# The end of a two-layer graph attention kernel: where the last weights are summed, where the first layer's rows are added, and in which order the last products run

## The chip, the cores and the metric

The kernel runs on one core of a Trainium2 chip. A core has TensorE (PE) for matrix products into PSUM, VectorE (DVE), ScalarE (ACT) and GpSimd (POOL) for everything elementwise, and SyncE (SP), which here issues DMAs. Each engine works through its own queue of instructions in order; semaphores make one engine wait for another. The metric is the device time of one execution in microseconds, as the median of several runs.

## The reference, cut to what matters

Two attention layers over a graph of 4096 nodes with 512 features. Each layer adds its input to its output and normalises every row. Only the second layer's end is touched here:

```python
q = jnp.einsum('nd,hdk->hnk', node_matrix, Wqs)
k = jnp.einsum('nd,hdk->hnk', node_matrix, Wks)
v = jnp.einsum('nd,hdk->hnk', node_matrix, Wvs)
scores = jnp.einsum('hqk,hmk->hqm', q, k) * kd ** (-0.5)
scores = scores + IDENTITY_BIAS * eye - MASK_VAL * (1.0 - adj)
att = jax.nn.softmax(scores, axis=-1)
return jnp.einsum('hqm,hmk,hko->qo', att, v, Wo)
...
x = _layernorm(x + _L1_gnn_ref(x, adj, ...), axis=-1)
```

There are 8 heads of 64 features. The softmax's denominator is a sum over all 4096 nodes, for every head and every row.

## The kernel before, in words

The second layer works on pairs of heads and groups of 512 rows: 8 groups `g` times 4 pairs of heads `m` give 32 `pairs`, and each runs over 32 tiles `j` of 128 neighbours. For one `(g, m, j)` TensorE computes the scores of 128 neighbours against 512 rows for two heads (`score`, L1138), ScalarE takes the exponential (L1549), and VectorE multiplies with the mask (L1552), which gives the weight tile `p`, 128 by 1024. Then TensorE multiplies `p` with the values into an accumulator `o` in PSUM (`products`, L1597). `step` takes up to three tiles `j` at once: it issues the scores of this batch, the weighing of this batch, and the products of the batch before.

The denominators need the sum of all 32 weight tiles of a pair. `add_up` plans it: for two neighbouring tiles either a DMA adds one onto the other (L1582) and GpSimd adds the result to `q_sum` (L1572), or GpSimd adds both. The plan is carried out later, by `Later`: `later.at(n, fn)` calls `fn` at the n-th `later.step()` from then on, and every `step` ends with one `later.step()`. Instructions stand in the engines' queues in the order in which this Python code issues them; nothing reorders them. At the end of a pair TensorE sums `q_sum` over the partitions with a matrix of ones, and the result's reciprocal is multiplied onto `o` (`divide`, or `divide_at_once` for the last pair), giving `on`. When a group's four pairs are done, `project` multiplies `on` with the output weights (four products per tile of 128 rows, one for each `m`), and `close1` adds the first layer's rows `y` (loaded by `load_y`), takes the row's mean and variance (`normal_factors`: two VectorE instructions, L510 and L512, then four small ones on GpSimd, L514 to L519), normalises on ScalarE (L1676) and writes the tile out.

In the last pair the ten weight tiles from `j` = 22 on are not given to GpSimd but put in the list `last_sum`. After the last batch VectorE adds six of these into one (five instructions, L1729) and TensorE sums the remaining four itself, together with `q_sum` and VectorE's sum (`all_sums`, L1603). At that point five tiles of rows are open: `tiles[-5]`, of the group before, and the four of the last group. Of these four, the products for `m` = 0, 1 and 2 can run early, and only the last one needs the last pair's `on`. The kernel also tests that all sums are in range (`all_in_range`), counts the partitions for which this holds with a tiny matrix product, and reads the number; if it is not 128, a general version would run.

PSUM has three buffers for scores (`s_ps`), which the last tiles' results use too, and one for `o` (`o1_ps`).

Of the kernel before, what the change touches and what calls it, by code (L numbers as in the profile page):

```python
# [13 lines left out]
ALU = mybir.AluOpType  # L14
# [415 lines left out]
def tile_gat_then_masked_attention(  # L430
# [91 lines left out]
    def all_in_range():  # L522
# [3 lines left out]
        for n, op in ((0, ALU.max), (2, ALU.min)):  # L526
            nc.vector.tensor_reduce(ends[:, 2 + n:4 + n],
                                    span[:, :, n:n + 2].rearrange("p g k -> p k g"), AX.X, op)
        nc.vector.tensor_reduce(ends[:, 0:1], total, AX.X, ALU.add)
        nc.vector.tensor_reduce(ends[:, 1:2], most, AX.X, ALU.add)  # L530
        for n, (value, limit, op) in enumerate((
                (ends[:, 2:3], F_MAX, ALU.is_le), (ends[:, 3:4], F_MAX, ALU.is_le),
                (ends[:, 4:5], -F_MAX, ALU.is_ge), (ends[:, 5:6], -F_MAX, ALU.is_ge),
                (ends[:, 0:1], SUM_MAX, ALU.is_le), (ends[:, 1:2], 1.0 / SUM_MIN, ALU.is_le))):
            nc.vector.tensor_scalar(ok[:, n:n + 1], value, limit, None, op0=op)
# [561 lines left out]
    with wait_by_tile("l1", 1) as l1, wait_by_tile("l1a", 2) as lp, \  # L1097
# [415 lines left out]
        with wait_by_tile("l1w", 2) as wp, wait_by_tile("l1o", 1, space=PSUM) as op:  # L1513
# [42 lines left out]
            def add_up(g, m, j):  # L1556
# [19 lines left out]
                elif at_end and i >= n - 5:  # L1576
                    last_sum.extend((a, b))
# [7 lines left out]
            last_sum = []  # L1585

# [72 lines left out]
            def project(g, t, s, ms=range(NP1)):  # L1659
                for m in ms:  # L1660
                    nc.tensor.matmul(s, on_t[g][:, m, t * P:(t + 1) * P], wo_sb[:, m, :],  # L1661
                                     start=(m == 0), stop=(m == NP1 - 1))
# [17 lines left out]

# [8 lines left out]
            def step(batch, extra_sum, extra_tile, wait=4):  # L1689
# [15 lines left out]
                for u in batch:  # L1705
                    add_up(*u)
                for g, m, j in last:
                    products(g, m, j)
# [6 lines left out]
                last[:] = batch  # L1715
                later.step()

            for n, (g, m) in enumerate(pairs):
                for js in per_pair if n + 1 < len(pairs) else last_pair:
# [4 lines left out]
            for t in tiles[-5:]:  # L1724
                load_y(*t)
            step([], None, None)
            later.step()
            for p in last_sum[1:-4]:
                nc.vector.tensor_tensor(last_sum[0], last_sum[0], p, op=ALU.add)  # L1729
            step([], None, tiles[-5], 2)  # L1730
            y_ps = ps.tile([P, HP, G], F32, name="s_ps")
            den_ps = ps.tile([P, HP, G], F32, name="s_ps")
            o_ps = op.tile([P, 2, G], F32, name="o1_ps")
            y_ps = [y_ps[:, 0, :], y_ps[:, 1, :], o_ps[:, 0, :], o_ps[:, 1, :]]
            for n in range(2):
                project(*tiles[n - GT], y_ps[n], range(NP1 - 1))
            all_sums([q_sum.pop(pairs[-1]), last_sum[0]] + last_sum[-4:], den_ps[:, 0, :])
# [52 lines left out]
```

## Time and profile before

| what | value |
|---|---|
| median of 3 runs (lowest to highest) | 3330.91 us (3329.23 to 3331.56) |
| profiled execution | 3330.41 us, span 3328.3 us |
| TensorE busy | 3301.2 us, 99% of the span |
| VectorE busy | 2484.2 us, 75% |
| GpSimd busy | 2167.3 us, 65% |
| ScalarE busy | 1949.1 us, 59% |
| GpSimd sum `q_sum<-q_sum,p` (L1572) | 538 times, mean 2561 ns |
| VectorE weighing `p<-s_ps,adjT` (L1552) | 896 times, mean 1217 ns |
| last score products end | 3286.8 us |
| last result on ScalarE begins | 3320.87 us |

The span runs from the first to the last instruction of the core; the execution's own time is somewhat longer. A group of instructions is named by its line in the kernel, the engine, the operation, and the tiles it writes and reads (`out<-in`). PEld is TensorE's loading of weights, which overlaps its products; one product of 32-bit numbers shows as two records. A record's duration begins when the instruction is issued to the engine[...]. "PEclk" is the granted clock of TensorE, 1.00 being full.

### The profile page before, as it was taken

The numbers are of one execution on the slowest core, as the hardware profiler recorded it, in microseconds if no ns is written. First come the engines' busy times: TensorE is split into PE (matmuls) and PEld (weight loads), VectorE is DVE, ScalarE is ACT, GpSimd is POOL, SyncE is SP. The second block draws the span as 40 slices with busy tenths as digits, with TensorE's granted clock in tenths as the row PEclk, the third lists the DMA queues.
The fourth block names the chain that finished last, engine by engine and source line by source line (L and its number), as shares of the span: only waits on it lengthen the run. The fifth ranks groups of instructions, "written<-read, shape, count | busy, mean of one in ns | idle before, by whom it ended". The sixth has DMA issues, their size and how long they took to land.

```text
span 3328.3 us, 67210 instructions
## 1 busy us (share of the span) xinstructions
PE 3301.2 (99%) x27160; PEld 1965.5 (59%) x27160; DVE 2484.2 (75%) x3189; ACT 1949.1 (59%) x2439; POOL 2167.3 (65%) x1599
## 2 busy tenths in 40 slices
PE   9999999999999999999999999999999999999998
PEld 8899999999999777733333333333333333333333
DVE  6789899899999676567767676676766767667676
ACT  1267868878776310156656556566565656656554
POOL 5630040040030243389999999999999999999996
PEclk9999999999999999999999999999999999999999
DMA  8988796686532443489888988879888799887984
GB/s 180 227 204 183 219 187 169 152 184 146 137 93 58 111 149 114 149 223 205 191 211 226 224 202 191 210 188 257 203 194 212 186 214 244 194 210 186 213 196 112
DMA packets 398992, 612.04 MB, mean 184 GB/s; under 512 B 167632, under 2 KB 248528, under 8 KB 398672
## 3 DMA queue, kind: packets, MB, share of 16 engines
q0 software_dynamic: 97520, 258.77, 42.6%
q1 hardware_dynamic: 299280, 345.88, 33.5%
q8 instruction: 215, 3.52, 0.4%
q10 hardware_dynamic: 1872, 3.02, 0.4%
q14 instruction: 105, 0.86, 0.1%
HBM read 315.87 MB, written 109.25 MB: 128 GB/s over the span
## 4 chain that ended last, share of the span: by engine, by line
PE 92%; POOL 3%; DMA 2%; DVE 1%; issue 1%; ACT 0%; ACTq 0%; POOLq 0%; DVEq 0%
PE o_ps L1087 27%; PE o_ps L1597 24%; PE s_ps L1138 24%; PE o_ps L846 5%; PE s_ps L1661 3%; PE s_ps L1298 2%; PE s_ps L1255 2%; DMA p<-p 2%; PE s_ps L1248 1%; PE x_ps L1255 1%; POOL q_sum L1572 1%; PE x_ps L1248 1%; PE s_ps L1616 1%; POOL p L1582 0%; POOL adjT L1214 0%
## 5 line engine op out<-in xcount | busy, mean ns | idle before, releaser
L1572 POOL TENSOR_TENSOR q_sum<-q_sum,p 128x1024 f32<-128x1024 f32 x538 | 1378.0, 2561 | 64.0 <-DMA p<-p 38.2
L1552 DVE TENSOR_TENSOR p<-s_ps,adjT 128x1024 f32<-128x1024 f32 x896 | 1043.9, 1217 | 470.1 <-ACT s_ps L1549 438.4
L1549 ACT ACTIVATE s_ps<-s_ps 128x1024 f32<-128x1024 f32 x1021 | 967.5, 1006 | 597.3 <-PE s_ps L1138 594.2
L1138 PE MATMUL s_ps<-q_sb,k_sb 64*64 64x512 f32 x8192 | 943.5, 589 | 2.8 <-DVE p L1552 2.7
L1597 PE MATMUL o_ps<-p,v_sb 64*64 64x512 f32 x8192 | 943.6, 590 | 0.0
L1087 PE MATMUL o_ps<-sup_t,p 128*128 128x129 f32 x8192 | 915.7, 275 | 1.2 <-DVE p L640 1.2
L1087 PEld LDWEIGHTS o_ps<-sup_t,p 128*128 128x128 f32 x8192 | 915.3, 192 | 1.7 <-DVE p L640 1.4
L640 DVE SCALAR_TENSOR_TENSOR p<-fr_t,dj,az 128x1024 f32<-128x1024 f32 x512 | 650.2, 1284 | 66.1 <-PE o_ps L1087 37.9
L1138 PEld LDWEIGHTS s_ps<-q_sb,k_sb 64*64 64x64 f32 x8192 | 312.4, 133 | 569.9 <-issue 453.7
L1597 PEld LDWEIGHTS o_ps<-p,v_sb 64*64 64x64 f32 x8192 | 310.2, 133 | 570.7 <-issue 560.4
L624 ACT ACTIVATE z<-fr_t,f 128x1024 fp8e4<-128x1024 f32 x512 | 557.9, 1146 | 102.1 <-DVE az L635 101.8
L1582 POOL DMA_DIRECT2D p<-p x412 | 438.4, 1302 | 10.1 <-PE o_ps L1597 9.2
L1063 POOL DMA_DIRECT2D agg<-base_d x32 | 29.1, 1217 | 386.8 <-DMA sup_t<-sup_d 204.7
L585 POOL COPY seen<-token 128x1 f32<-128x1 f32 x24 | 10.9, 455 | 356.8 <-DVE token L583 356.8
L1552 DVE TENSOR_TENSOR p<-s_ps,md 128x1024 f32<-128x1024 f32 x128 | 150.8, 1218 | 67.0 <-ACT s_ps L1549 63.6
L635 DVE TENSOR_TENSOR az<-adjT,z 128x512 int32<-128x512 int32 x256 | 175.4, 685 | 2.9 <-ACT z L624 1.8
L600 ACT ACTIVATE adjT<-stage 128x1024 fp8e4<-128x1024 bf16 x128 | 131.2, 1055 | 17.0 <-DMA stage<-adj_d 16.7
L1661 PE MATMUL s_ps<-wo_sb,on 128*128 128x512 f32 x240 | 110.8, 604 | 0.0
L1631 ACT ACTIVATE r<-r_h 32x256 f32<-32x256 f32 x248 | 102.3, 413 | 2.9
L1277 POOL TENSOR_TENSOR v_sb<-v_sb,p 128x1024 f32<-128x1024 f32 x8 | 20.6, 2569 | 95.9 <-DVE v_sb L1283 52.4
L1049 ACT ACTIVATE agg<-o_ps,rinv 128x128 f32<-128x128 f32 x128 | 42.0, 370 | 69.8 <-DVE den L1042 45.9
L1322 ACT ACTIVATE v<-s_ps 128x256 f32<-128x256 f32 x28 | 10.8, 384 | 117.6 <-PE s_ps L1298 102.5
(274 smaller groups left out, 2257.3 us busy)
## 6 DMA issues: line engine op xcount, KB each, us to landing
p<-p POOLq DMA_DIRECT2D x412, 512.0 KB, 9.1
k_sb<-k_d SPq DMA_DIRECT2D x128, 512.0 KB
v_sb<-v_d SPq DMA_DIRECT2D x128, 512.0 KB
adj_d<-in_adj_dram POOLq DMA_DIRECT2D x32, 1024.0 KB, 11.0
sup_t<-sup_d SPq DMA_DIRECT2D x120, 258.0 KB
fr_t<-fr_d SPq DMA_DIRECT2D x16, 1024.0 KB
adjT_d<-adjT SPq DMA_DIRECT2D x32, 512.0 KB
adjT<-adjT_d SPq DMA_DIRECT2D x32, 512.0 KB
```

The lines of the kernel that those rows point to most:

```text
L624: nc.scalar.activation(z[:, k, :], fr_t[w, h][:, 0, :], AF.Sign, bias=fs[j // GT][:, 0, (j + k) % GT, h:h + 1], saturate=False)
L635: nc.vector.tensor_tensor(az.bitcast(I32), adjT[w, j // CJ][:, j % CJ:j % CJ + 2, :].bitcast(I32), z.bitcast(I32), op=ALU.bitwise_and)
L640: nc.vector.scalar_tensor_tensor(p, fr[:, 1, :], dj[j // GT][:, j % GT, h:h + 1], az_t[w, h, j // 2][:, j % 2, :], op0=ALU.max, op1=ALU.mult)
L846: nc.tensor.matmul(out[:, t * HD:(t + 1) * HD], xb[:, c, t * P:(t + 1) * P], wb[:, c, :], start=not more and t == 0 and c == 0, stop=c == ...
L1087: nc.tensor.matmul(o[t // BK][:, t % BK, :], p[:, t * P:(t + 1) * P], s, start=(j == 0 and t % BK == 0), stop=(j == NT - 1), skip_group_ch ...
L1138: nc.tensor.matmul(s[c:c + MS, e, :], k[r, a + c:a + c + MS], qt[g, m][r, :], start=True, stop=True)
L1549: nc.scalar.activation(s, s, AF.Exp, scale=float(KD) ** -0.5)
L1552: nc.vector.tensor_tensor(p, s, keep[:, None, :].to_broadcast([P, HP, G]), op=ALU.mult)
L1572: nc.gpsimd.tensor_tensor(q, q, p, op=ALU.add)
L1582: later.at(2, lambda: nc.gpsimd.dma_start(a, b, accum_op=ALU.add))
L1597: nc.tensor.matmul(o[c, n, :], v[r, j % CH, c], p[r, e, :], start=(j == 0), stop=(j == NT - 1))
L1661: nc.tensor.matmul(s, on_t[g][:, m, t * P:(t + 1) * P], wo_sb[:, m, :], start=(m == 0), stop=(m == NP1 - 1))
```

## The change

Four things change, all behind the last weighings or near them.

1. The list `last_sum` is summed by `gather` on VectorE: one sum after the second-last batch, five after the last batch is weighed, two more after the last pair's products. The last weight tile of all (`j` = 31) is left out of these and added to `q_sum` on GpSimd, planned five steps later by `add_up`. TensorE then sums only `q_sum` and the gathered tile.
2. The first layer's rows of the last four tiles are copied by ScalarE into the PSUM accumulators, and `project` adds its products onto them (`onto`); `close_in_place` therefore has no addition of `y`, takes mean and variance from PSUM, and normalises from PSUM, the last tile on VectorE and the others on ScalarE.
3. The products of `tiles[-5]` now come before the last pair's products, and the parts of the last four tiles are interleaved with their last products in another order. The closing of `tiles[-5]` comes after the gathering.
4. The range test is cut in two: what is known early is tested before the last sums (`in_range_so_far`), the rest after the first of the four tiles has been closed. Four of the five loads of `y` are issued two steps earlier, the fifth where it was.

```diff
--- before.py
+++ after.py
@@ -519,20 +519,26 @@
         nc.gpsimd.tensor_scalar(nb, nb, -1.0, None, op0=ALU.mult)
         return rs, nb
 
-    def all_in_range():
+    def in_range_so_far():
 
         ok = small.tile([P, 8], F32, name="ok")
         ends = small.tile([P, 6], F32, name="ends")
         for n, op in ((0, ALU.max), (2, ALU.min)):
             nc.vector.tensor_reduce(ends[:, 2 + n:4 + n],
                                     span[:, :, n:n + 2].rearrange("p g k -> p k g"), AX.X, op)
+        for n, (value, limit, op) in enumerate((
+                (ends[:, 2:3], F_MAX, ALU.is_le), (ends[:, 3:4], F_MAX, ALU.is_le),
+                (ends[:, 4:5], -F_MAX, ALU.is_ge), (ends[:, 5:6], -F_MAX, ALU.is_ge))):
+            nc.vector.tensor_scalar(ok[:, n:n + 1], value, limit, None, op0=op)
+        return ok, ends
+
+    def all_in_range(known):
+
+        ok, ends = known
         nc.vector.tensor_reduce(ends[:, 0:1], total, AX.X, ALU.add)
         nc.vector.tensor_reduce(ends[:, 1:2], most, AX.X, ALU.add)
-        for n, (value, limit, op) in enumerate((
-                (ends[:, 2:3], F_MAX, ALU.is_le), (ends[:, 3:4], F_MAX, ALU.is_le),
-                (ends[:, 4:5], -F_MAX, ALU.is_ge), (ends[:, 5:6], -F_MAX, ALU.is_ge),
-                (ends[:, 0:1], SUM_MAX, ALU.is_le), (ends[:, 1:2], 1.0 / SUM_MIN, ALU.is_le))):
-            nc.vector.tensor_scalar(ok[:, n:n + 1], value, limit, None, op0=op)
+        for n, value, limit in ((4, ends[:, 0:1], SUM_MAX), (5, ends[:, 1:2], 1.0 / SUM_MIN)):
+            nc.vector.tensor_scalar(ok[:, n:n + 1], value, limit, None, op0=ALU.is_le)
         all_ok = small.tile([P, 1], F32, name="all_ok")
         nc.vector.tensor_reduce(all_ok, ok[:, 0:6], AX.X, ALU.min)
         return all_ok
@@ -1574,6 +1580,8 @@
                 if i == 0:
                     later.at(1, first)
                 elif at_end and i >= n - 5:
+                    if j == NT - 1:
+                        later.at(5, lambda: add(b))
                     last_sum.extend((a, b))
                 elif i % 8 == 7:
                     later.at(2, lambda: add(a))
@@ -1583,6 +1591,11 @@
                     later.at(5, lambda: add(a))
 
             last_sum = []
+
+            def gather(count):
+                for p in last_sum[1:1 + count]:
+                    nc.vector.tensor_tensor(last_sum[0], last_sum[0], p, op=ALU.add)
+                del last_sum[1:1 + count]
 
             def products(g, m, j):
                 if j == 0:
@@ -1656,10 +1669,11 @@
                     den = wp.tile([P, G], F32, name="den1", bufs=1)
                     nc.scalar.activation(den, src, AF.Copy, accum_out=sums[:, n:n + 1])
 
-            def project(g, t, s, ms=range(NP1)):
+            def project(g, t, s, ms=range(NP1), onto=False):
                 for m in ms:
                     nc.tensor.matmul(s, on_t[g][:, m, t * P:(t + 1) * P], wo_sb[:, m, :],
-                                     start=(m == 0), stop=(m == NP1 - 1))
+                                     start=(m == 0 and not onto), stop=(m == NP1 - 1),
+                                     skip_group_check=onto)
 
             def load_y(g, t):
                 y_t[g, t] = wp.tile([P, D], F32, name="y1", bufs=5)
@@ -1677,7 +1691,25 @@
                     nc.sync.dma_start(out[i * P:(i + 1) * P, :], y)
                 later.at(wait, normalise)
 
-
+            def close_in_place(g, t, s, vector=False):
+                i = g * GT + t
+                y = y_t.pop((g, t))
+                st = small.tile([P, 6], F32, name="bn_st")
+                nc.vector.bn_stats(st, s)
+                mv = small.tile([P, 2], F32, name="bn_mv")
+                nc.vector.bn_aggr(mv, st)
+                rs = small.tile([P, 1], F32, name="bn_rs")
+                nc.gpsimd.tensor_scalar(rs, mv[:, 1:2], EPS, None, op0=ALU.add)
+                nc.gpsimd.tensor_tensor(rs, rs, minus_half, op=ALU.pow)
+                if vector:
+                    nc.vector.tensor_scalar(y, s, mv[:, 0:1], rs, op0=ALU.subtract,
+                                            op1=ALU.mult)
+                else:
+                    nb = small.tile([P, 1], F32, name="bn_nb")
+                    nc.gpsimd.tensor_tensor(nb, mv[:, 0:1], rs, op=ALU.mult)
+                    nc.gpsimd.tensor_scalar(nb, nb, -1.0, None, op0=ALU.mult)
+                    nc.scalar.activation(y, s, AF.Identity, bias=nb, scale=rs)
+                nc.sync.dma_start(out[i * P:(i + 1) * P, :], y)
 
             per_pair = [list(range(j, min(j + NB, NT))) for j in range(0, NT, NB)]
             n_short = 5
@@ -1704,6 +1736,11 @@
                     divide(*extra_sum, extra[:, 0, :])
                 for u in batch:
                     add_up(*u)
+                all_products()
+                last[:] = batch
+                later.step()
+
+            def all_products():
                 for g, m, j in last:
                     products(g, m, j)
                 for g, m, j in last:
@@ -1712,44 +1749,65 @@
                         o = o_t.pop((g, m))
                         nc.scalar.activation(o_sb[g, m], o[:, 0, :], AF.Copy)
                         nc.vector.tensor_tensor(o_sb[g, m], o_sb[g, m], o[:, 1, :], op=ALU.add)
-                last[:] = batch
-                later.step()
 
             for n, (g, m) in enumerate(pairs):
-                for js in per_pair if n + 1 < len(pairs) else last_pair:
+                for k, js in enumerate(per_pair if n + 1 < len(pairs) else last_pair):
                     whole = len(js) == NB
                     step([(g, m, j) for j in js],
                          None if whole or n < 1 else pairs[n - 1],
                          None if whole or n < NP1 + 1 else tiles[n - NP1 - 1])
-            for t in tiles[-5:]:
-                load_y(*t)
-            step([], None, None)
+                    if n + 1 == len(pairs):
+                        left = len(last_pair) - 1 - k
+                        if left == 2:
+                            for t in tiles[-5:-1]:
+                                load_y(*t)
+                        elif left == 0:
+                            load_y(*tiles[-1])
+                        elif left == 1:
+                            gather(1)
+            extra = ps.tile([P, HP, G], F32, name="s_ps")
+            project(*tiles[-5], extra[:, 1, :])
+            y_ps = ps.tile([P, HP, G], F32, name="s_ps")
+            y_ps = [y_ps[:, 0, :], y_ps[:, 1, :]]
+            for n in range(2):
+                nc.scalar.activation(y_ps[n], y_t[tiles[n - GT]], AF.Copy)
+            gather(5)
+            all_products()
             later.step()
-            for p in last_sum[1:-4]:
-                nc.vector.tensor_tensor(last_sum[0], last_sum[0], p, op=ALU.add)
-            step([], None, tiles[-5], 2)
-            y_ps = ps.tile([P, HP, G], F32, name="s_ps")
+            gather(len(last_sum) - 2)
+            close1(*tiles[-5], extra[:, 1, :], 2)
             den_ps = ps.tile([P, HP, G], F32, name="s_ps")
             o_ps = op.tile([P, 2, G], F32, name="o1_ps")
-            y_ps = [y_ps[:, 0, :], y_ps[:, 1, :], o_ps[:, 0, :], o_ps[:, 1, :]]
-            for n in range(2):
-                project(*tiles[n - GT], y_ps[n], range(NP1 - 1))
-            all_sums([q_sum.pop(pairs[-1]), last_sum[0]] + last_sum[-4:], den_ps[:, 0, :])
+            y_ps += [o_ps[:, 0, :], o_ps[:, 1, :]]
+            for n in range(2, GT):
+                nc.scalar.activation(y_ps[n], y_t[tiles[n - GT]], AF.Copy)
+            for _ in range(5):
+                later.step()
+            known = in_range_so_far()
+
+            def part(n):
+                project(*tiles[n - GT], y_ps[n], range(NP1 - 1), onto=True)
+
+            def rest(n):
+                project(*tiles[n - GT], y_ps[n], [NP1 - 1], onto=True)
+
+            part(0)
+            part(1)
+            all_sums([q_sum.pop(pairs[-1]), last_sum[0]], den_ps[:, 0, :])
             divide_at_once(*pairs[-1], den_ps[:, 0, :])
-            for n in range(GT):
-                if n + 2 < GT:
-                    project(*tiles[n + 2 - GT], y_ps[n + 2], range(NP1 - 1))
-                project(*tiles[n - GT], y_ps[n], [NP1 - 1])
-                if n == GT - 2:
-                    continue
-                if n == GT - 1:
-                    all_ok = all_in_range()
-                    close1(*tiles[n - 1 - GT], y_ps[n - 1], 1)
-                close1(*tiles[n - GT], y_ps[n], 1)
-                later.step()
-            count = den_ps[0:1, 1, 0:1]
-            nc.tensor.matmul(count, all_ok, ones[:, 0:1], start=True, stop=True)
-            nc.vector.tensor_copy(counted, count)
+            part(2)
+            rest(0)
+            part(3)
+            close_in_place(*tiles[-GT], y_ps[0])
+            all_ok = all_in_range(known)
+            for n in range(1, GT):
+                rest(n)
+                if n == 1:
+                    count = den_ps[0:1, 1, 0:1]
+                    nc.tensor.matmul(count, all_ok, ones[:, 0:1], start=True, stop=True)
+                close_in_place(*tiles[n - GT], y_ps[n], n == GT - 1)
+                if n == 1:
+                    nc.vector.tensor_copy(counted, count)
             later.flush()
```

## The prediction, made before the changed kernel was run

> **What bounds the kernel now.** The page's table of engines and its chain of work come first. TensorE is busy for almost the whole span and holds 92% of the chain, so nothing but the end of the kernel, where TensorE stops being the bound, can be moved by this change.
>
> ```profile
> span 3328.3 us, 67210 instructions
> PE 3301.2 (99%) x27160; PEld 1965.5 (59%) x27160; DVE 2484.2 (75%) x3189; ACT 1949.1 (59%) x2439; POOL 2167.3 (65%) x1599
> PE 92%; POOL 3%; DMA 2%; DVE 1%; issue 1%; ACT 0%; ACTq 0%; POOLq 0%; DVEq 0%
> ```
>
> Next, the same chain in order of time for the last 67 us (start, us, what). TensorE carries it to 3292.0; then it is VectorE's five sums of the last weights (L1729), TensorE's sums over them (L1603), TensorE's last products (L1661), and from 3313.7 VectorE, GpSimd and ScalarE closing the last tiles.
>
> ```profile
> 3286.83 5.20 PE o_ps L1597 x48
> ...
> 3292.68 0.69 DVE o_sb L1714
> 3293.36 1.62 DVE p L1729
> ...
> 3295.01 3.26 DVE p L1729
> ...
> 3302.09 4.50 PE s_ps L1603 x40
> 3306.59 2.77 PE o_ps L1661 x6
> ...
> 3320.33 0.19 POOL bn_nb L518
> ...
> 3320.87 0.81 ACT y L1676
> ```
>
> The last ScalarE result ends at 3321.68, its output DMA is issued at 3321.71, and the span ends 6.6 us later. I keep those 6.6 us.
>
> Third, the time lines of VectorE and GpSimd one by one, since the change spreads sums over both.
>
> ```profile
> 3293.28 1.69 DVE L1729 TENSOR_TENSOR p<-p,p 128x1024 f32<-128x1024 f32 x1
> 3295.01 3.25 DVE L1729 TENSOR_TENSOR p<-p,p 128x1024 f32<-128x1024 f32 x1
> 3298.29 1.23 DVE L1729 TENSOR_TENSOR p<-p,p 128x1024 f32<-128x1024 f32 x1
> 3291.54 2.35 POOL L1572 TENSOR_TENSOR q_sum<-q_sum,p 128x1024 f32<-128x1024 f32 x1
> 3294.01 3.16 POOL L1572 TENSOR_TENSOR q_sum<-q_sum,p 128x1024 f32<-128x1024 f32 x1
> ```
>
> The same VectorE sum takes 1.23 us when GpSimd is idle and up to 3.25 us beside a GpSimd sum, which itself goes from 2.35 to 3.16. The ends show turns being taken: GpSimd ends at 3293.89, VectorE at 3294.97, GpSimd at 3297.17 (2.20 later), VectorE at 3298.26 (1.09 later). One sum of each costs 3.29 us of common time.
>
> **What the skill says of it.** The Trainium skill, page "SBUF — State Buffer", section "Who interferes with whom", says that a VectorE instruction with two SBUF inputs and a GpSimd instruction that reads SBUF exclude each other for a whole instruction, whichever came first. The rows above agree (3.29 us a pair), and so does L1552, which reads PSUM and one SBUF operand and keeps its mean of 1217 ns beside busy GpSimd. I go by the trace's 2.20 and 1.09. The page "TensorE: Matmul & The Clock Gate", section "Part 1: The HAM clock gate", says that an idle window of about 3.4 us halves TensorE's clock until a busy one has passed. The stretches around the one long gap of TensorE, near the start, agree: 3.50 us idle, then one stretch of 3.42 us at clock 0.50 with 10 matmuls where the next 3.42 us hold 17 (stretch, PE busy and count, ..., clock third from the end).
>
> ```profile
> 10.81:14.31 3.50, 0.00 (x1) 0.00 (x1) 2.70 (x6) 1.88 (x2) 1.26 (x1) 1.00 1.06 254
> 14.87:18.29 3.42, 3.42 (x10) 2.70 (x9) 3.42 (x4) 0.60 (x1) 2.69 (x3) 0.50 1.06 267
> 18.29:21.71 3.42, 3.42 (x17) 3.01 (x16) 0.24 (x2) 1.61 (x3) 2.69 (x12) 1.00 1.20 188
> ```
>
> **Part 1, the sums.** Before, ten last weights: five VectorE sums join the first six; TensorE sums four more itself. After, eight VectorE sums (one, then five, then two) and one more on GpSimd, of the last weight. In queue order:
>
> *The first sum* stands in VectorE's queue between the weighings of the last two batches, where VectorE idles 1.52 us (3284.77 to 3286.29). GpSimd is in a sum there that can only have begun when its DMA issue (L1582, 3283.39 + 1.17) ended at 3284.56; it ends at 3286.95. So VectorE's sum waits and ends about 1.09 later, 3288.04. Behind it are the three last weighings (3.49 us, L1552): they end at 3291.5, not 3289.78. For those wait the last products; they are covered, because the first tile's 8 matmuls (L1661, 0.43 each, 3.44 us) now stand before them, so they begin at 3292.84. GpSimd's `on` product (L1635) waits some 0.25 us.
>
> *The five sums* start at 3291.5. GpSimd then still has two sums, of three L1572 left after L1635. Two pairs at 3.29 and three sums alone at 1.25: 3291.5 + 6.6 + 3.8 = 3301.9.
>
> *Then* VectorE's `o_sb` (0.66, L1714; its products ended by 3295.4 and ScalarE's copy by 3296.0, both early) to 3302.6, two sums (2.5) to 3305.1, and the first closed tile's add, statistics and aggregate (L1671, L510, L512: 3302.04 to 3303.58 before, 1.54) to 3306.65.
>
> *GpSimd's sum of the last weight* is due three steps later than the tile's closing, so in GpSimd's queue it stands behind that tile's four small operations (L514 to L519), which wait for L512. This is the wait that the change adds. Four operations take 1.56 (3303.58 to 3305.14 before): 3308.2; the sum 2.35 (nothing with two SBUF inputs runs beside it): 3310.55. Queued behind it on GpSimd are only the last tiles' factors; TensorE waits for it.
>
> *TensorE's sums over partitions* fall from 48 instructions to 16. Ten groups of four took 4.50, so 0.43 a group and 0.2: four groups take 1.9. They end at 3312.5, against 3306.59: **5.9 us later**. TensorE's own work ahead of them is unchanged in amount (8 + 24 + 12 records, to 3300.7), so it idles for 9.9 us.
>
> **Part 2, the clock.** That gap is three times the 3.50 us that halved the clock. At half clock the four groups take about 1.7 more. How long the low clock lasts depends on where the windows fall: 1.7 us of wall time if a half-busy window is enough, up to 6.8 if a whole busy one is needed. Half of this is lost: 0.85 to 3.4, I take **2.1**. Past the sums it delays the remaining matmuls, which from the second tile on are on the path.
>
> **Part 3, the tail**, counted from the end S of the sums (3306.59 before; the output was issued at S + 15.12). The reciprocals and products (L1653, L1654) are unchanged, to S + 5.0. Four y adds (L1671, 0.69 each) go: y is copied into PSUM by ScalarE beforehand (four copies at about 0.60, as L1713; two near 3291, two near 3304, in ScalarE's idle time; if that cover were gone, 2.4). Statistics read PSUM; I price them as from SBUF, 0.69 (PSUM-reading adds cost 0.68, like the others); between 0.6 and 0.8. Four limits and two reductions of the range test (about 0.4) move into the wait for part 1: free. Tile 0's statistics end at S + 5.8. ScalarE's totals still come at S + 6.2 (it waits for the last reciprocal, as now: 18.7 us on L1653), so the shortened test ends at S + 6.75. TensorE's last product of tile 1 ends at S + 7.06, as now; statistics to S + 8.0. From there GpSimd binds: 1.54 a tile, tile 1 to 9.6, tile 2 (statistics 9.1) to 11.1, tile 3 with two operations instead of four to 12.05. VectorE normalises it (no such row; like L1671 0.69, between 0.4 and 0.8): 12.8, issue S + 12.84. **2.3 us gained.** The output DMAs remain one a tile; loading four rows sooner and one later stays in SP's idle time.
>
> **Sum:** 5.9 + 2.1 - 2.3 = +5.7 us. On the profiled execution's own 3330.41 (its span 3328.3 and 2.1 around it) that is 3336.1; the runs' median lies 0.5 above it, so **3336.6**, 0.17% above before. A difference of 0.2% is 6.7 us, about what a measurement of this kernel can tell from none, so the likeliest case is a small loss that falls just inside it.
>
> **Rivals.** (a) On the other side: the engines don't queue, and the last weight's sum is not late. VectorE's first sum fits its idle 1.52 us, five end by 3296.0, `o_sb` at 3296.75, two more 3299.25, statistics 3300.8, GpSimd's four 3302.35, its sum 3304.7, S at 3306.65: no later than before, and the tail's 2.3 remain: 3328.6. It decides as long as GpSimd's last sum ends by about 3306.9 at full clock. For it: that most of GpSimd's work is ahead of these sums; against it: the rows of 1.69 and 3.25. (b) The clock stays halved to the end: the 20 last matmul records, 8.8 us, become 17.4, statistics and factors follow (2.7), S is 3314.2, so issue at 3334.3, +12.6: 3343.5. Against it: the clock came back after one window near the start, with TensorE as busy. (c) The turns fall worse (GpSimd behind by its first sum: +0.5) and the low clock lasts two windows (+1.3) : +7.5 to +9, about 3339.5. For it: nothing fixes where windows fall. (d) The accumulation on ScalarE's copies does not hold TensorE: the copies of tiles 2 and 3 wait only for `o_sb`, 3302.6, and have over 6 us; a rival only in name.
>
> **How the numbers follow.** My case 0.70, spread +4 to +7.6 on its own (3334.9 to 3338.5); (a) 0.14; (c) 0.10; (b) 0.06. Range 3332 to 3341: it leaves out most of (a) and all of (b). Slower by over 0.2%: a quarter of my case (0.17), (b) and (c): 0.33. Faster by over 0.2% would need 6.7 us, more than any case gives: 0.02. The rest 0.65.
>
> **What would show it.** Right: L1729's successor with sums near 2 to 3.3 us beside L1572; the last L1572 starting right after an L519 near 3308; TensorE idle some 10 us before L1603; a stretch at 0.50 after it; the last VectorE result about 12.8 us after L1603 (more by the low clock). Wrong: a last L1572 that starts before L514, VectorE sums all at 1.23, or no low clock.

## The result and the profile after

The changed kernel takes 3340.78 us (median of 8 runs, 3337.24 to 3341.36), the kernel before, run beside it, 3330.26 us (8 runs, 3327.04 to 3331.56). The ratio is 1.003, with a 95% interval of 1.0021 to 1.0038: slower by 7 to 13 us, more than the 0.2% that count as no change. Forecast were 3336.6 us with a range of 3332 to 3341, so the median lies 0.2 us inside the range; the likeliest class, within 0.2%, is not the one that came. The profiled execution took 3340.41 us, its span is 3338.4 us, 10.1 more than before.

The page of the changed kernel, the span, the engines and the chain by engine:

```profile
span 3338.4 us, 67150 instructions
PE 3301.7 (99%) x27128; PEld 1964.8 (59%) x27128; DVE 2489.7 (75%) x3189; ACT 1949.9 (58%) x2442; POOL 2169.4 (65%) x1598
PE 92%; POOL 2%; DMA 2%; DVE 2%; issue 1%; ACT 0%; ACTq 0%; POOLq 0%; DVEq 0%
```

TensorE's busy time is within 0.5 us of before, though the sums over partitions on it fell from 48 instructions to 16; so the ten microseconds are time in which it stands still, and some in which it runs slowly. Where, the chain of the changed kernel shows in order of time (start, us, what):

```profile
3290.76 1.17 DVE p L1597
...
3291.95 3.27 DVE p L1597
...
3295.24 3.26 DVE p L1597
...
3306.87 0.24 POOL bn_nb L519
3307.10 2.31 POOL q_sum L1578
...
3309.46 3.66 PE s_ps L1616 x16
...
3320.48 0.79 ACT y L1711
...
3321.31 1.14 PE s_ps L1674 x2
...
3326.50 0.79 ACT y L1711
...
3327.33 2.09 PE o_ps L1674 x2
...
3331.34 0.81 DVE y L1705
```

Before, TensorE was on the chain from 3302.09 (sums) to 3313.67 (last products) and then handed over to the others for good. Now VectorE's gathering (L1597) and GpSimd's last sum (L1578), directly behind a tile's factor (L519), stand ahead of TensorE's sums (L1616). And twice after that the chain goes back from ScalarE's normalisation (L1711) to a *product* of TensorE (L1674), 0.04 us after the normalisation ends. The chain of before has no such step.

The time lines of VectorE and GpSimd, one by one:

```profile
3284.03 3.33 DVE L1597 TENSOR_TENSOR p<-p,p 128x1024 f32<-128x1024 f32 x1
3287.28 3.47 DVE L1558 TENSOR_TENSOR p<-s_ps,md 128x1024 f32<-128x1024 f32 x3
3290.68 10.33 DVE L1597 TENSOR_TENSOR p<-p,p 128x1024 f32<-128x1024 f32 x5
3301.53 2.48 DVE L1597 TENSOR_TENSOR p<-p,p 128x1024 f32<-128x1024 f32 x2
3305.64 0.22 POOL L514 TENSOR_SCALAR bn_ve<-bn_mv 128x1 f32<-128x1 f32 x1 [8.23 <-DVE ends L527]
3306.87 0.24 POOL L519 TENSOR_SCALAR bn_nb<-bn_nb 128x1 f32<-128x1 f32 x1
3307.07 2.34 POOL L1578 TENSOR_TENSOR q_sum<-q_sum,p 128x1024 f32<-128x1024 f32 x1
```

The first gathered sum takes 3.33 us and pushes the three last weighings back. GpSimd stands idle for 8.23 us in front of L514 while the sum that TensorE needs is queued four instructions behind it. What TensorE and the others then waited for (engine, line, releaser: us, times, longest):

```profile
PE s_ps L1616 <- POOL q_sum L1578: 9.0, 1, 9.0
...
PE o_ps L1674 <- ACT y L1711: 3.7, 1, 3.7
...
PE s_ps L1674 <- ACT y L1711: 2.0, 1, 2.0
```

And two stretches of time (us, then busy time and count on PE, PEld, DVE, ACT and POOL, clock third from the end):

```profile
3309.46:3313.10 3.64, 3.64 (x17) 0.70 (x17) 0.00 (x0) 0.00 (x0) 0.00 (x0) 0.53 0.01 5
...
3321.30:3332.20 10.90, 4.37 (x8) 1.18 (x8) 3.49 (x8) 1.55 (x2) 3.19 (x10) 0.74 0.20 75
```

In the first the sums over partitions run at about half the clock; in the second the clock falls again, and the last product takes 2.07 us for two records instead of some 1.0.

For the comparison of kernels one anchor serves, since the work before it differs by a microsecond or two from one execution to the next: the end of the weighing of `j` = 28 on VectorE, at 3284.77 before and 3284.11 after. S is the end of TensorE's sums over partitions, T the end of the last result.

| | before | after | difference |
|---|---|---|---|
| anchor to S | 21.82 | 28.96 | +7.1 |
| S to T | 15.09 | 19.09 | +4.0 |
| T to the end of the span | 6.64 | 6.27 | -0.4 |
| sum | 43.55 | 54.31 | +10.8 |

With the anchor itself 0.66 us earlier this is the span's +10.1. Two thirds of the loss lie ahead of S, where the forecast had put the whole of it; one third lies in the tail, where a gain had been forecast.

### The profile page after: what moved, and what is told of

The parts are those of the page before. It is cut to its first block, busy times and chain, and to the rows that moved or that the text cites. A ratio compares the mean times of both kernels' runs of the same rounds, so it can differ in the third digit from the quotient of the medians.

```text
span 3338.4 us, 67150 instructions
## 1 busy us (share of the span) xinstructions
PE 3301.7 (99%) x27128; PEld 1964.8 (59%) x27128; DVE 2489.7 (75%) x3189; ACT 1949.9 (58%) x2442; POOL 2169.4 (65%) x1598
## 4 chain that ended last, share of the span: by engine, by line
PE 92%; POOL 2%; DMA 2%; DVE 2%; issue 1%; ACT 0%; ACTq 0%; POOLq 0%; DVEq 0%
PE o_ps L1093 27%; PE o_ps L1610 25%; PE s_ps L1144 25%; PE o_ps L852 5%; PE s_ps L1674 3%; PE s_ps L1304 2%; PE s_ps L1261 2%; DMA p<-p 2%; PE s_ps L1254 1%; PE x_ps L1261 1%; PE x_ps L1254 1%; PE s_ps L1629 1%; POOL q_sum L1578 0%; POOL adjT L1220 0%; POOL p L1590 0%
## 5 line engine op out<-in xcount | busy, mean ns | idle before, releaser
L1578 POOL TENSOR_TENSOR q_sum<-q_sum,p 128x1024 f32<-128x1024 f32 x539 | 1379.0, 2558 | 65.9 <-DMA p<-p 40.1
L1590 POOL DMA_DIRECT2D p<-p x412 | 438.7, 1304 | 10.1 <-PE o_ps L1610 9.2
L1674 PE MATMUL s_ps<-wo_sb,on 128*128 128x512 f32 x240 | 111.2, 605 | 2.0 <-ACT y L1711 2.0
```

What stands on the lines that cost most here:

```text
L1578: nc.gpsimd.tensor_tensor(q, q, p, op=ALU.add)
L1590: later.at(2, lambda: nc.gpsimd.dma_start(a, b, accum_op=ALU.add))
```

## The experiments

The theory after the result has two parts. *Ahead of S:* VectorE and GpSimd take turns, GpSimd's last sum stands behind the closed tile's factors, and the gap halves the clock. *Behind S:* the accumulators of two tiles are the halves of one PSUM tile, and the program orders what touches one half after what touched the other. By closing in place, ScalarE's normalisation, which comes late because it waits for GpSimd's factors, is now such a touch; before, it was VectorE's early addition of `y`. The rivals: the tail is late only because TensorE's queue has its products behind the closings, or because TensorE's clock is low there; and the gap in front of S costs by its length alone, or by the clock alone. That two engines hinder each other in PSUM while both work on it is no rival: TensorE stood still from 3319.27 on, and the normalisation that it waited for began only at 3320.48.

All runs, with the three distances of the table above (us):

| run | median | before beside it | ratio (95%) | anchor to S | S to T | T to end |
|---|---|---|---|---|---|---|
| changed kernel | 3340.78 | 3330.26 | 1.0030 (1.0021 to 1.0038) | 28.96 | 19.09 | 6.27 |
| e1 products first | 3336.91 | 3329.49 | 1.0023 (1.0014 to 1.0032) | 28.69 | 15.77 | 6.44 |
| e2 GpSimd's sum early | 3335.52 | 3329.49 | 1.0018 (1.0011 to 1.0024) | 23.97 | 19.08 | 6.68 |
| e3 both | 3333.31 | 3329.49 | 1.0011 (1.0004 to 1.0017) | 23.97 | 15.91 | 6.31 |
| e4 sums on TensorE | 3328.98 | 3329.49 | 0.9998 (0.9990 to 1.0006) | 20.78 | 15.75 | 6.42 |
| e5 statistics first | 3335.15 | 3330.17 | 1.0015 (1.0008 to 1.0021) | 28.76 | 13.06 | 7.73 |
| e6 combination | 3327.86 | 3330.17 | 0.9993 (0.9985 to 1.0002) | 20.10 | 13.93 | 7.78 |
| e7 filled gap | 3339.86 | 3330.17 | 1.0030 (1.0019 to 1.0041) | 27.30 | 18.93 | 6.62 |
| e8 fewer GpSimd sums | 3336.23 | 3330.17 | 1.0017 (1.0010 to 1.0023) | 24.74 | 19.23 | 6.45 |
| e9 other halves | 3335.27 | 3329.81 | 1.0018 (1.0010 to 1.0026) | 27.32 | 14.99 | 6.71 |
| e10 second output queue | 3334.81 | 3329.81 | 1.0013 (1.0006 to 1.0020) | 28.95 | 13.06 | 6.94 |
| e11 combination, two queues | 3325.50 | 3329.68 | 0.9987 (0.9980 to 0.9993) | 20.05 | 13.93 | 6.51 |

### e1: all last products ahead of the closings

`part(n)` issues the first three products of tile n, `rest(n)` its last one.

```diff
             part(2)
             rest(0)
+            rest(1)
             part(3)
+            rest(2)
+            rest(3)
             close_in_place(*tiles[-GT], y_ps[0])
             all_ok = all_in_range(known)
+            count = den_ps[0:1, 1, 0:1]
+            nc.tensor.matmul(count, all_ok, ones[:, 0:1], start=True, stop=True)
             for n in range(1, GT):
-                rest(n)
-                if n == 1:
-                    count = den_ps[0:1, 1, 0:1]
-                    nc.tensor.matmul(count, all_ok, ones[:, 0:1], start=True, stop=True)
                 close_in_place(*tiles[n - GT], y_ps[n], n == GT - 1)
-                if n == 1:
+                if n == 2:
                     nc.vector.tensor_copy(counted, count)
```

> The changed kernel with all four last products (L1674) issued ahead of the closings of the last four tiles, in the order part 2, rest 0, rest 1, part 3, rest 2, rest 3; the count's product follows the range test. Theory A (the halves of one PSUM tile wait for each other: the last product of tile 1 waits for ScalarE's reading of tile 0, that of tile 3 for ScalarE's reading of tile 2): the two waits of 2.0 and 3.7 us on ScalarE vanish, the last result comes about 13 us after the end of the sums over partitions instead of 19.05, so some 6 us less than the changed kernel, about 3334.5 us or 1.0013 of before. Rival B (the tail is long because TensorE's clock was low): the order of instructions changes nothing, within 1 us of the changed kernel, 1.003 of before.

The last result comes 15.77 us after S: 3.3 sooner, and not the 6 that the theory gave; a low clock alone would have left it at 19. TensorE's two waits are gone, but VectorE has taken them over. Its time line in this run:

```profile
3320.86 0.70 DVE L1698 BATCH_NORM_STATS2 bn_st<-s_ps 128x6 f32<-128x512 f32 x1 [1.41 <-ACT y L1711]
...
3325.69 0.70 DVE L1698 BATCH_NORM_STATS2 bn_st<-o_ps 128x6 f32<-128x512 f32 x1 [3.09 <-ACT y L1711]
```

The statistics of tiles 1 and 3 wait for ScalarE's normalisation of tiles 0 and 2. Both only read PSUM, and each its own half. So the order holds between reads of two engines too, and TensorE's queue was not the cause but the first place where it showed.

### e2: GpSimd's last sum planned two steps later instead of five

```diff
                     if j == NT - 1:
-                        later.at(5, lambda: add(b))
+                        later.at(2, lambda: add(b))
```

> The changed kernel with GpSimd's sum of the last weight planned two steps ahead instead of five, so that it stands before the four small operations of the first closed tile in GpSimd's queue. Theory A (the sum is late because it stands behind operations that wait for VectorE's statistics): it ends near 3300.7 instead of 3309.4; VectorE's sums, one more of them in turn with GpSimd, end near 3306.1 instead of 3304.0 and now bind; the sums over partitions end near 3307.5 (TensorE idle 4 to 5 us, clock full or half) instead of 3313.1: 5 to 6 us less than the changed kernel, about 3335.2 us or 1.0015 of before. Rival B (the exclusion of the two engines is what costs, wherever the sum stands): VectorE's sums lose what GpSimd gains, at most 2 us less than the changed kernel.

S comes 5.0 us sooner and the tail is as long as before (19.08). GpSimd's sum, now behind no factors, ends early; but it is a third one beside VectorE's gathering, which becomes 12.36 us for five sums, 2.03 more. What TensorE waits for now is VectorE (TensorE's time line of this run):

```profile
3300.40 1.07 PE L1616 MATMUL s_ps<-q_sum,ones 128*32 128x512 f32 x8 [0.34 <-POOL q_sum L1578]
3305.73 1.93 PE L1616 MATMUL s_ps<-p,ones 128*32 128x512 f32 x8 [4.27 <-DVE p L1597]
```

Still S is 2.2 us later than before (23.97 against 21.82), 0.9 of it for the second row's low clock: the place in the queue was the larger part of the loss ahead of S, but the work given to VectorE alone is enough to be late.

### e3: e1 and e2 together

The edits of e1 and e2, unchanged.

> Both edits, the products ahead of the closings and GpSimd's sum planned two steps ahead. If the two causes are separate, their gains add: 11 to 12 us less than the changed kernel, about 3329 us or 0.9997 of before. If they share a cause (TensorE's low clock that follows its idling), the gain is that of one alone, about 6 us.

The span measured from the anchor is 46.19 us, 8.1 less than in the changed kernel: 5.0 from S and 3.2 from the tail, and 0.0 from the end. (Against the kernel before beside it the median gained 6.7 us; the profiled execution is 2.0 us faster than this run's median.) The two parts add, so they are separate; the sum falls short of what was expected mostly by what e1 fell short.

### e4: the sums left on TensorE

e1, with no sum of `j` = 31 on GpSimd and no last two gathered sums:

```diff
-                    if j == NT - 1:
-                        later.at(5, lambda: add(b))
...
-            gather(len(last_sum) - 2)
...
-            all_sums([q_sum.pop(pairs[-1]), last_sum[0]], den_ps[:, 0, :])
+            all_sums([q_sum.pop(pairs[-1])] + last_sum[1:] + last_sum[:1], den_ps[:, 0, :])
```

> The products ahead of the closings, and the last three weight tiles summed over partitions by TensorE itself, in the order GpSimd's sum, these three, VectorE's sum last; no GpSimd sum of the last weight and only six sums on VectorE. Theory A: TensorE has no gap ahead of these sums, VectorE's sum is ready near 3301.0, the sums end about 4.5 us after TensorE's part of the products at 3300.5, so at 3305.0, 8 us sooner than in the changed kernel and about 1 us sooner than before; the clock stays full up to there; with a tail of about 13 us this is some 3 us below the kernel before: 3327 us or 0.999. Rival: if the tail of 13 us is wrong because of another wait between the halves of a PSUM tile, 3330 or above.

TensorE goes from its products (to 3302.03) into its sums without a gap:

```profile
3301.95 1.06 PE L1614 MATMUL s_ps<-q_sum,ones 128*32 128x512 f32 x8
3302.84 3.62 PE L1614 MATMUL s_ps<-p,ones 128*32 128x512 f32 x32
```

S lies 1.0 us ahead of that of the kernel before, in which TensorE summed one tile more. With 15.75 us behind S the kernel is as fast as before (0.9998), though it still has the wait that e1 moved to VectorE. So it was the way of summing that made S late; the ScalarE copies, the other order of products and the earlier loads, which e4 keeps, cost nothing visible there.

### e5: all statistics ahead of all normalisations

e1, with `close_in_place` cut into a part that issues statistics and factors and a part that normalises and writes out:

```diff
-            close_in_place(*tiles[-GT], y_ps[0])
+            factors = [statistics(*tiles[-GT], y_ps[0])]
...
             for n in range(1, GT):
-                close_in_place(*tiles[n - GT], y_ps[n], n == GT - 1)
+                factors.append(statistics(*tiles[n - GT], y_ps[n], n == GT - 1))
...
+            for n in range(GT):
+                normalise_in_place(*tiles[n - GT], y_ps[n], factors[n], n == GT - 1)
```

> The changed kernel with the products ahead of the closings, as in the first experiment, and in addition the statistics of all four tiles issued ahead of all four normalisations. In the first experiment the wait did not vanish but moved: VectorE's statistics of tiles 1 and 3 waited 4.5 us for ScalarE's reading of tiles 0 and 2. Theory A (any two engines that touch the two halves of one PSUM tile are put in the order of the program, reads too): with the statistics ahead, none of them waits for ScalarE, and GpSimd's factors, 1.54 us a tile, bind: last result about 13 us after the end of the sums over partitions (19.05 in the changed kernel, about 15.6 in the first experiment): some 2.7 us less than the first experiment, about 1.0014 of before. Rival B: GpSimd's factors bind already, no gain over the first experiment, 1.0023.

The last result ends 13.06 us after S, as expected, and no statistics wait for ScalarE any more. Those of tiles 1 and 3 in VectorE's time line of this run:

```profile
3318.89 0.69 DVE L1696 BATCH_NORM_STATS2 bn_st<-s_ps 128x6 f32<-128x512 f32 x1
...
3321.85 0.68 DVE L1696 BATCH_NORM_STATS2 bn_st<-o_ps 128x6 f32<-128x512 f32 x1
```

This is the tail that the prediction had worked out (12.8) for the changed kernel. Of the 6.0 us gained, 1.5 are given back at the very end, which is now 7.73 us behind the last result; the last two outputs are issued 0.98 us apart here, 1.53 in the kernel before. e10 takes that up.

### e9: neighbours in order get halves of different PSUM tiles

e1 and e5 change the order of instructions. This one leaves it alone and changes only which accumulators share a PSUM tile: 0 with 2 and 1 with 3, instead of 0 with 1 and 2 with 3.

```diff
-            y_ps = [y_ps[:, 0, :], y_ps[:, 1, :]]
-            for n in range(2):
+            y_ps = [y_ps[:, 0, :], None, y_ps[:, 1, :], None]
+            for n in (0, 2):
                 nc.scalar.activation(y_ps[n], y_t[tiles[n - GT]], AF.Copy)
...
-            y_ps += [o_ps[:, 0, :], o_ps[:, 1, :]]
-            for n in range(2, GT):
+            y_ps[1], y_ps[3] = o_ps[:, 0, :], o_ps[:, 1, :]
+            for n in (1, 3):
                 nc.scalar.activation(y_ps[n], y_t[tiles[n - GT]], AF.Copy)
```

> The changed kernel with one difference: the accumulators of the last four tiles are dealt out so that neighbours in order share no PSUM tile (tiles 0 and 2 in one, 1 and 3 in the other, instead of 0 and 1, 2 and 3). Theory, halves of one PSUM tile are ordered against each other: tile 1's last product no longer waits for ScalarE's normalisation of tile 0; tile 2's last product now waits for it, but by then it is nearly done (0.5 to 1 us), and tile 3's waits for the normalisation of tile 1, which is earlier than that of tile 2. Counted from the end S of the sums over partitions the last result ends at about S + 14 instead of S + 19.1, 5 us sooner; TensorE has part of tile 1's early products in its gap, so that the sums may also run at the full clock, up to 1.7 us sooner. Together 4 to 7 us faster than the changed kernel. Rival, each last product waits for the ScalarE normalisation of the tile before it wherever that tile lies: S + 19 stays.

TensorE's time line of this run:

```profile
3302.69 5.49 PE L1674 MATMUL o_ps<-wo_sb,on 128*128 128x512 f32 x6 [5.09 <-ACT o_ps L1783]
...
3314.61 3.60 PE L1674 MATMUL o_ps<-wo_sb,on 128*128 128x512 f32 x8
...
3319.38 1.12 PE L1674 MATMUL s_ps<-wo_sb,on 128*128 128x512 f32 x2 [1.05 <-ACT y L1711]
3321.56 1.82 PE L1674 MATMUL o_ps<-wo_sb,on 128*128 128x512 f32 x2 [1.06 <-ACT y L1711]
```

Tile 1's last product no longer waits (it is in the second row). Tile 2's waits 1.05 us for tile 0's normalisation, tile 3's 1.06 for tile 1's, each for the neighbour in its own PSUM tile; in the changed kernel it was tile 1's that waited 2.04 us and tile 3's that waited 3.71. The last result comes 14.99 us after S, 4.1 sooner; the rival, that each product waits for the closing before it, gave 19. The sharing of a PSUM tile is the cause of the tail's loss. The median is 5.5 us above its kernel before, where the changed kernel's is 10.5 above. Tile 1's three early products now fall into TensorE's gap (first row: they wait 5.09 us for ScalarE's copy of `y` into their accumulator), and the sums behind them run at the full clock: S is 1.6 us sooner.

The Trainium skill, page "PSUM — Partial Sum Buffer", section "PSUM bank collisions raise a hardware error", asks for guards between engines by bank and quadrant; by its section "Specifications (TRN2)" a bank holds 512 f32 a partition, which is one of these halves. The rows of e1 and e9 show the program guarding the whole PSUM tile, two banks by that figure, so more than this rule asks. A finer guard was not tried. The kernel opens both PSUM pools through its helper `wait_by_tile`, with `reuse_waits="tile"`; no run changes this setting, so whether it has a part in the order stays open.

### e7: TensorE's gap filled

Ten extra products without use for the result, in front of the sums over partitions:

```diff
             part(0)
             part(1)
+            for _ in range(10):
+                nc.tensor.matmul(den_ps[:, 1, :], on_t[pairs[-1][0]][:, 0, 0:P], wo_sb[:, 0, :],
+                                 start=True, stop=True)
             all_sums([q_sum.pop(pairs[-1]), last_sum[0]], den_ps[:, 0, :])
```

> The changed kernel with ten products more (20 records, 8.6 us) that TensorE makes into an unused PSUM half in its gap of 9 us ahead of the sums over partitions; their results are not used. Theory A (the gap halves TensorE's clock): the clock stays full, the sums over partitions take 1.9 us instead of 3.66, and nothing else moves before them: about 1.8 us less than the changed kernel, 1.0025 of before. Rival B (the sums take 3.66 us for another reason, such as reading tiles just written): no change.

TensorE's time line of this run:

```profile
3306.28 1.07 PE L1616 MATMUL s_ps<-q_sum,ones 128*32 128x512 f32 x8 [0.44 <-POOL q_sum L1578]
3307.16 1.04 PE L1616 MATMUL s_ps<-p,ones 128*32 128x512 f32 x8
```

The sums take 1.93 us instead of 3.61 and S is 1.66 sooner from the anchor, with the same start (25.38 against 25.35). So that much is the clock's, and the rest of S's delay is the gap itself. The tail keeps its 18.93 us and its two waits. By the times alone (1.0030, 1.0019 to 1.0041) the run decides nothing, since 1.7 us lie within its interval; the verdict rests on the trace. It agrees with the Trainium skill's page "TensorE: Matmul & The Clock Gate", section "Part 1: The HAM clock gate", by which an idle window halves the clock: 9.0 us idle gave 0.53 over the sums, the filled gap the full clock.

### e8: GpSimd's sums of four weights left out

The neighbour tiles 18 to 21 are not added to the denominators, so GpSimd has no sum beside VectorE's gathering:

```diff
-                    later.at(5, lambda: add(a))
+                    if not (at_end and j >= 19):
+                        later.at(5, lambda: add(a))
```

> The changed kernel with the last two GpSimd sums of the earlier weights (neighbours 18 to 21) left out, so these four weight tiles are missing from the last pair's denominators; everything else is as in the changed kernel. Theory A (VectorE's and GpSimd's sums exclude each other): VectorE's five sums take 1.23 us each instead of two at 3.25, all that follows comes 4.1 us sooner: about 3336.7 us or 1.0019. Rival B (VectorE's sums are slow for another reason, TensorE's or ScalarE's traffic): the two sums keep 2 us or more, gain under 1 us.

The group of VectorE's sums behind the weighings (count, then busy us and mean ns):

```profile
L1598 DVE TENSOR_TENSOR p<-p,p 128x1024 f32<-128x1024 f32 x7 | 8.6, 1224 | 0.2
```

All seven at 1224 ns, where two of the changed kernel's took 3.26. S is 4.2 us sooner (4.1 expected), the tail unchanged. The two long sums were GpSimd's neighbours in time and nothing else.

### e6, e10 and e11: a version from the parts, and its last output

e6 takes e5's tail, GpSimd's sum at two steps, and leaves the middle of the list to TensorE:

```diff
-                        later.at(5, lambda: add(b))
+                        later.at(2, lambda: add(b))
...
-            gather(len(last_sum) - 2)
...
-            all_sums([q_sum.pop(pairs[-1]), last_sum[0]], den_ps[:, 0, :])
+            all_sums(last_sum[1:-1] + [q_sum.pop(pairs[-1]), last_sum[0]], den_ps[:, 0, :])
```

> Products first and statistics first, GpSimd's sum of the last weight planned two steps ahead, and the two weight tiles that VectorE added last left to TensorE: its order is these two, GpSimd's sum, VectorE's sum last. Theory: TensorE goes on without a gap (under 1 us) from the early products to these sums, the clock stays full, the sums end about 1 us sooner than with three tiles left to TensorE, and the tail is about 13 us: 3.5 to 4 us below that experiment and before, about 3325.7 us or 0.9988. Rival: VectorE's fifth sum, in turn with one more GpSimd sum, is late by 2 us and TensorE waits for it; then about 3327.5, 0.9994.

S comes 1.7 us sooner than in the kernel before. The tail is 13.93, not 13.06, because VectorE, closing `tiles[-5]` and testing ranges, begins the reciprocals only 1.4 us after S. The median is 2.3 us below that of before, but the interval reaches 1.0002; and the end again takes 7.78 us.

e10 is e5 with one change, e11 is e6 with the same one:

```diff
-                nc.sync.dma_start(out[i * P:(i + 1) * P, :], y)
+                (nc.scalar if vector else nc.sync).dma_start(out[i * P:(i + 1) * P, :], y)
```

> The kernel with all four tiles' statistics ahead of all normalisations (where the span ended 7.7 us after the last result, against 6.3 to 6.6 in kernels whose last two outputs lie further apart), with one difference: the last tile's output is issued from ScalarE's DMA queue instead of SyncE's. If the 1.3 us at the end come from two outputs close together in one queue, the span ends 6.3 to 6.6 us after the last result. If they come from what the two outputs share beyond the queue, or from anything else, it stays at 7.7.

> The kernel with the sums on TensorE, GpSimd's last sum planned two steps after the weighing, all last products ahead of the closing and statistics ahead of normalisations (it measured 0.9993 of the kernel before, 0.9985 to 1.0002, and its span ended 7.8 us after the last result), with the last tile's output issued from ScalarE's DMA queue instead of SyncE's. If one shared queue costs part of those 7.8 us, as the run with the other queue shows (6.9 for 7.7), the span ends about 7.0 us after the last result and the time is some 0.8 us shorter: 3327 us, 0.999 of before. If that 6.9 was only chance, 7.8 and no difference.

With the last output in a queue of its own, issued as close to the one before it as ever (0.99 us), the span ends 6.94 us after the last result instead of 7.73, and 6.51 instead of 7.78. e10 alone would leave it open, as its value lies between the two that were expected and its median is 5.0 us above the kernel before beside it, as e5's is; e11 has nearly all of the difference. Each of these distances comes from one profiled execution. So the time given back at the end is most likely that of two outputs of 256 KB close together in one queue; what in the queue takes it, the runs do not show. e11 lies below both kernels: 0.9987 of before (0.9980 to 0.9993), 4 us, which is clear of 1 but less than the 0.2% that count as no change.

## Why the prediction was right or wrong

**The sums: right, 5.5 for 5.9 us.** The first gathered sum did wait for GpSimd (3.33 us), and the last weighing ended 1.6 us later than before against the anchor (1.7 forecast). Of the five sums two took 3.27 and 3.26 us and the others 1.23, as worked out. GpSimd's last sum started directly behind L519, at 3307.07, which is 22.96 us after the anchor (23.4 forecast). At the full clock S would have been 27.30 us after the anchor, which e7 shows; before it was 21.82. e8 shows the turns, e2 the place in the queue.

**The clock: right, 1.7 for 2.1 us, and then a second time.** The sums lost 1.7 us. The low clock lasted 3.44 us, inside the 1.7 to 6.8 us that the prediction allowed and shorter than its middle value, so that it was back before the products behind them: at 1.00 over the next 8.2 us. Another 1.0 us was lost on the very last product (2.07 us), behind a gap of 3.71 us which the prediction did not have; it is counted with the tail.

**The tail: wrong, a loss of 4.0 us for a gain of 2.3.** The step that failed is "TensorE's last product of tile 1 ends at S + 7.06, as now". It ended at S + 9.4, since it first waited 2.04 us for ScalarE's normalisation of tile 0, which itself waits for four operations of GpSimd. From there the numbers of the prediction hold, 2.3 us late, up to the factors of tile 2 (S + 13.4 for 11.1). Then the same happens to tile 3: its product waits 3.71 us and runs at half the clock, so its factors are ready at S + 18.2 instead of 12.05. The rest is small: normalising from PSUM on VectorE took 0.81 us, not 0.69. Statistics from PSUM took 0.69 to 0.70, as priced.

"As now" was the mistake: the order between halves was there already, and the waits of the kernel before had a row for it, between the two products of one PSUM tile.

```profile
PEld s_ps L1661 <- DVE y L1671: 0.3, 1, 0.3
```

It cost 0.3 us because the last one to touch the other half was VectorE's addition, which comes first in a closing. The change took this addition away and thereby made ScalarE's normalisation the last one, which ends 3.2 us after its closing began (3318.08 to 3321.27 for tile 0), where the addition, coming first, had taken 0.7. The prediction priced the removed instruction and did not ask what else it had done: it had freed PSUM. e5 gives the tail without that order, 13.06 us for the 12.8 forecast, so little else was missing from that step.

**The rivals.** (a), not slower, fails at its condition: GpSimd's last sum ended at 3309.4, not by about 3306.9. (b), the clock low to the end, did not come. (c) had nearly the time, 3339.5, but not the reasons: the turns were no worse than taken, and the clock was back 3.44 us after the sums began. (d) stayed in name only: the copies of tiles 2 and 3 ended at 3302.87, and the first product onto them began at 3313.00, without a wait for them. None had the tail. That the time still fell into the range is luck: the upper end was there for a slower sum and a longer low clock, neither of which came, and the time reached it by the tail, which was forecast with the wrong sign. The right range and the wrong class come from this: ahead of S the forecast was 8.0 us and 7.1 came; behind it the forecast was -2.3 and +4.0 came, 6.3 more. With -0.4 at the end and -0.7 at the anchor the forecast +5.7 becomes the measured +10.1.

## What to carry to other kernels

Before a computation is moved into PSUM to save a copy or an addition, ask what that instruction released: who touches the same PSUM tile next, in either half, on any engine, and behind which chain the new last reader stands. When a sum is planned "some steps later", list what then stands ahead of it in its engine's queue and what that waits for; four tiny operations held 2.3 us of work for 8 us here. A sum taken from TensorE, where it cost 0.9 us, and given to VectorE, where it costs 1.23 us alone and 3.26 beside GpSimd, gains nothing where TensorE then stands waiting for it.

## What the runs showed that was not expected

- Reads of two halves of one PSUM tile by two engines were ordered by the program (VectorE 3.09 us behind ScalarE in e1). VectorE began to wait at 3319.45, and ScalarE began to read only at 3320.05, so it is an order that is kept and not a hindrance while both read.
- TensorE's clock halved a second time after idle stretches of 2.04 and 3.71 us with some 2.3 us of work between them, and doubled the time of the last product (2.07 us for about 1.0). One long gap is not needed: in e9 two gaps of 1.05 and 1.06 us with 1.1 us of work between them came ahead of a last product of 1.82 us at a clock of 0.58.
- The time from the last result to the end of the span was 6.3 to 6.7 us where the last two outputs lay over 1.5 us apart or in two queues (6.9 in one such run), and 7.7 to 7.8 us where they lay 0.98 us apart in one queue.
